# Writing the attention's work in its final order on every engine of a fused transformer block

## The chip, the cores and the metric

The kernel runs on one core of a Trainium2 chip. A core has five engines that run side by side, each with its own stream of instructions: TensorE (PE, matrix products into PSUM), VectorE (DVE), ScalarE (ACT), GpSimd (POOL) and SyncE (SP), which here only issues DMA transfers. The metric is the device time of one launch in microseconds (us). Every stream is fixed when the program is compiled; engines wait for each other by semaphores.

## The reference

One transformer block on a sequence of 2048 rows of width 1024, all in float32:

```python
x = x + layernorm(attention(layernorm(x)))     # 16 heads of 64, rotary q and k, causal softmax
x = x + layernorm(ffn(layernorm(x)))           # silu(x Wg^T) * (x Wu^T), then Wd^T; 2752 inner columns
# q, k, v = y @ Wq, y @ Wk, y @ Wv;  out = softmax(q k^T / 8, masked) v;  attention = out @ Wo
# Wg, Wu, Wd come as 4-bit codes: NF4[codes] * scales, one scale for each block of 64
```

## The kernel before

**Numbers.** Every float32 operand of a product is split into a rounded high part and a remainder (`split`, L125: a ScalarE copy, then a VectorE subtraction), and a product takes three matmuls, high by high, high by remainder, remainder by high.

**Stages.** A start-up makes the normalised and transposed first 512 rows and q, k, v of four head pairs. Then comes one long loop over *steps* (L651) which holds the whole attention and much of what surrounds it; this is what the change is about. After it come the last four projection tiles, the feed-forward's gate and up products, and its down product.

**The step loop.** A unit of work is 128 keys of one head against 512 queries; there are 640 units, one a step, from step 0, and 12 steps ahead of them. In each step things are written in this order of rank: loads of q, k and v for later heads (rank 0, `load_q`, `load_k`, `load_v`); the unit's scores s, two or three matmuls into one of three PSUM banks "S", and their exponential on ScalarE (rank 1, `probabilities`); one matmul for the row maxima of a later head, into a bank "T", with its VectorE reduction (rank 2, `maxima`); filling (rank 3); the weighted sum o of the unit three steps back (rank 4, `weighted`); the split of s into pw (rank 5, `parts`), which frees the bank of s.

**Filling.** `rest` is a Python generator that yields one matmul at a time, or GAP to end the step's share; the table `FILL` says how many matmuls are to be spent by which step. It makes q, k and v of the other head pairs (`qkv`: for each of q, k, v a run of 24 matmuls, then the copy t1, the weight split for the next group, the rotary products t1 and sh on VectorE and GpSimd, the split hl, and its store to DRAM), `values` (transposes of v), and, from about step 440 on, the first 12 tiles of the output projection (`project_out`, each two runs of 24 matmuls; its input is `attended`, the attention's sums af times their reciprocals rt, split into ah and af; its output goes through `residual`, two layer norms and the residual sum). `other_x` runs beside it and makes the other rows' normalised transposes. `looked_up` turns 4-bit codes into weights with eight linear pieces; four such lookups are put into the last steps.

**Buffers.** Tags name rings of SBUF slots (`SLOTS`, L72). The ones that matter here: f4, four slots of 4 KB a partition (weight rows wf and wof, hl, vo, af, ah, mp), pb, two slots (x rows, y, x1), pw, three slots (tables, rt, xs, lookup codes), xc and pa (x tiles, weights).

**Order.** The matmuls are chained by `chain` (L418) in the order written. For every other engine and for the DMA queue, a scheduler picks the order when the program is compiled: it replays the program with modelled durations and takes, on each engine, what is ready by its model, earlier written work first. The order it picks is then fixed: an engine that comes to an instruction whose input isn't there stands still.

Of the kernel before, what the change touches and what calls it, by code (L numbers as in the profile page):

```python
# [20 lines left out]
S = 2048  # L21
# [18 lines left out]
FILL = ((-12, 0), (14, 304), (130, 912), (290, 1520), (430, 2128), (438, 2128), (643, 2704))  # L40
# [19 lines left out]
def block_kernel(ctx, tc, x, wq, wk, wv, wo, gu_codes, gu_scales, d_codes, d_scales, cos_sin, out):  # L60
# [56 lines left out]

    def mm3(o, w, xx, first, last):

        r = T.matmul(o, lhsT=w[:, 0], rhs=xx[:, 0], start=first, stop=False)  # L120
        T.matmul(o, lhsT=w[:, 0], rhs=xx[:, 1], start=False, stop=False)  # L121
        T.matmul(o, lhsT=w[:, 1], rhs=xx[:, 0], start=False, stop=last)  # L122
        return r
# [5 lines left out]
    def ln_stats(row):  # L129
        st = small.tile([P, 2, 6], F32, tag="st", name="st")  # L130
        for i in range(2):
            V.bn_stats(st[:, i, :], row[i])
        mv = small.tile([P, 2], F32, tag="mv", name="mv")
        V.bn_aggr(mv, st.rearrange("p a b -> p (a b)"))
        ve = small.tile([P, 1], F32, tag="ve", name="ve")
        V.tensor_scalar(ve, mv[:, 1:2], EPS, None, ALU.add)  # L136
        rs = small.tile([P, 1], F32, tag="rs", name="rs")
        G.tensor_tensor(rs, ve, nhalf, ALU.pow)  # L138
        nb = small.tile([P, 1], F32, tag="nb", name="nb")
        V.tensor_scalar(nb, mv[:, 0:1], rs, -1.0, ALU.mult, ALU.mult)  # L140
        return mv[:, 0:1], rs, nb

# [42 lines left out]

    def x_rows(r, tag):

        xt = slot(tag, [P, E], F32, "xt")
        load(xt, x[r * P : (r + 1) * P, :])
        mean, rs, _ = ln_stats(halves(xt))  # L190
        V.tensor_scalar(xt, xt, mean, rs, ALU.subtract, ALU.mult)
        return xt
# [7 lines left out]
    def load_x(c, kps):  # L200
        tiles = []
        for kp in kps:
            tiles.append(slot(X_TAGS[c][kp], [P, 4, 2, 2, P], FR, "xc"))
            load(f32(tiles[-1]), xd[c][:, kp])
        return tiles
# [8 lines left out]
    def make_x(c, t, xt):  # L214

        for g in range(0, KE, 4):
# [6 lines left out]
            load(xd[c][:, g // 2 : g // 2 + 2, t], f32(xs))  # L223
            yield GAP

    def qkv(m, c, ws, xs, tab, ramp=False, following=None, before=(), after_n=None):


        cs = slice(c * 512, (c + 1) * 512)
        for n in range(3):  # L230
            w = ws[n]
            o = bank("S" if ramp and n != 1 else "F", "qkv")
            if following:
                wf = load_w(n, following[1])
# [10 lines left out]
            if following:  # L245
                following[0][n] = split_w(wf, following[2])
            if n < 2:
# [5 lines left out]
                hl = slot("f4", [P, 2, 512], FR, "hl")  # L253
                split(hl[:, 0, :], hl[:, 1, :], t1)
                if n == 0:
                    load(qs[m][:, :, cs], f32(hl))
                else:
                    for a in range(2):
                        load(ks[m][a][:, :, cs].rearrange("a d s -> d a s"), f32(hl[a * D : (a + 1) * D]))
            if after_n:  # L260
                after_n(n)
# [4 lines left out]
        def values():  # L266
# [5 lines left out]
            for a in range(2):  # L272
                split(vo[:, a, :, 1], vo[:, a, :, 0], src[:, a])
            load(
                vs[m][:, :, 4 * c : 4 * c + 4].rearrange("a p t n -> p a (t n)"),
                f32(vo.rearrange("p a t l d -> p a (t l d)")),
            )
            done.add((m, c))
# [16 lines left out]
    def startup():  # L295
        nonlocal behind
        for m in range(STARTUP):
            ws[m + 2] = [None] * 3 if m + 2 <= STARTUP else None
            following = ws[m + 2] and (ws[m + 2], m + 2, ("w", "pa", "w", "w")[m])
            behind = yield from qkv(m, 0, ws[m], xs, tab, True, following, behind)  # L300
# [4 lines left out]
    def looked_up(codes, s0, s1, rows, line0="ol"):  # L305
# [6 lines left out]
        load(sc[D:], s1.partition_broadcast(D))  # L312
        l0 = slot(line0, [P, 512], F32, "l0")
# [12 lines left out]
        V.scalar_tensor_tensor(m, line(L6), 0.0, m, ALU.min, ALU.min)  # L326
        l8 = line(L8)
        V.tensor_tensor(p, l8, line(L10), ALU.max)
        V.tensor_tensor(p, p, line(L12), ALU.max)
        V.tensor_tensor(p, p, line(L14), ALU.max)  # L330
        V.scalar_tensor_tensor(m, p, 0.0, m, ALU.max, ALU.add)
        V.tensor_tensor(m, m, sc, ALU.mult)
        return m

    def gate_up_weights(it, line0="ol"):
# [4 lines left out]
        def columns_of(k0):  # L340
# [3 lines left out]
            m = looked_up(  # L344
# [4 lines left out]
        return (it, wt, w), [partial(columns_of, k0) for k0 in range(0, KE, kk)]  # L349
# [35 lines left out]
    def load_q(n, h, J):  # L385

        m, r, cs = h // 2, h % 2, slice(J * 512, J * 512 + 512)
        assert (m, J) in done, (h, J, step, spent)
# [35 lines left out]
    mx_of, later = {}, []  # L424

    def maxima(h, J, j, i):
# [12 lines left out]
        if (j, i) == (3, J):  # L439
# [12 lines left out]
            later.append((3, row))  # L452
# [30 lines left out]
    def weighted(u, h, J, kb):  # L483
# [13 lines left out]
        load(at[J][:, h], y)  # L497
        done.add(("at", h, J))
        if h == 2 * KE - 1 and J < NC - 1:
            reciprocals(J)  # L500

    def prep_wo(k, tag):
        wf = slot("f4", [P, E], F32, "wof")
        load(wf, wo[k * P : (k + 1) * P, :])
        t = slot(tag, [P, 2, E], FR, "wo")
        A.copy(t[:, 0], wf)
        (V, G)[k % 2].tensor_tensor(t[:, 1], wf, f32(t[:, 0]), ALU.subtract)
        return t[:, :, :512], t[:, :, 512:]
# [3 lines left out]
    def reciprocals(J):  # L512
# [3 lines left out]
        V.reciprocal(r, r)  # L516
        load(rcp[J].rearrange("h (a d) -> (h a) d", a=8), r)

    def attended(t):
# [6 lines left out]
        for a in range(2):  # L526
            one = rcp[t // 4][:, cs].rearrange("(k a) n -> a k n", a=2)[a : a + 1]
            load(rt[a * D : (a + 1) * D], one.to_broadcast([D, KE, P]))
        V.tensor_tensor(rt, f32(af), rt, ALU.mult)
        hi = slot("f4", [P, KE, P], FR, "ah")  # L530
        split(hi, af, rt)
        return hi, af

    def project(t, y, a2, beside):

        for n in range(2):
            o = bank("FT"[n] if beside else "FSS"[(2 * t + n) % 3], "pj")
            for k in range(KE):
                yield T.matmul(o, lhsT=a2[0][:, k], rhs=wot[k][n][:, 0], start=k == 0, stop=False)  # L539
                yield T.matmul(o, lhsT=a2[0][:, k], rhs=wot[k][n][:, 1], start=False, stop=False)  # L540
                yield T.matmul(o, lhsT=a2[1][:, k], rhs=wot[k][n][:, 0], start=False, stop=k == KE - 1)  # L541
            A.copy(y[:, n * 512 : (n + 1) * 512], o)  # L542
            yield GAP

    def residual(t, y, xt):

        rows = slice(t * P, (t + 1) * P)
        load(xt, x[rows, :])
        normalize(y, y, ln_stats(halves(y)))
        G.tensor_tensor(xt, xt, y, ALU.add)  # L550
        load(x1d[rows, :], xt)
        normalize(y, xt, ln_stats(halves(xt)))

    def project_out(t, a2, beside):
        y = slot("pb", [P, E], F32, "y")
        yield from project(t, y, a2, beside)
        residual(t, y, slot("pb", [P, E], F32, "x1"))
        load(yd[t], y)
# [3 lines left out]
    def other_x():  # L562
        tiles = [(c, t) for c in range(1, NC) for t in range(4)]
        ready = [x_rows(4, "pb")]
        for n, (c, t) in enumerate(tiles):
            ready += [x_rows(4 * i + j, "pb") for i, j in tiles[n + 1 : n + 2]]
            yield GAP
            while c > 1 and (0, c - 1) not in done:
                yield GAP
            yield from make_x(c, t, ready.pop(0))  # L570
            if t == 3:
                done.add(("x", c))

    def rest():

        xs_, tab_, w, values, ahead = xs, tab, ws[STARTUP], behind, []
        for g in range(STARTUP, len(groups)):
            m, c = groups[g]
            if m == 0:
                while ("x", c) not in done:  # L580
                    yield GAP
                xs_ = [*ahead, *load_x(c, range(len(ahead), 4))]
# [3 lines left out]
            if m == KE - 2 and ("x", c + 1) in done:  # L586
                ahead = load_x(c + 1, range(2))
            if g == len(groups) - 2:
                wot[0] = prep_wo(0, "pa")
            following = [None] * 3  # L590
            last = g + 1 == len(groups)

            def wo_after(n):
                wot[n + 1] = prep_wo(n + 1, "w")

            one = qkv(
                m, c, w, xs_, tab_, False, None if last else (following, groups[g + 1][0], "w"), values, wo_after if last else None
            )
# [7 lines left out]
        for k in range(4, KE):  # L606
            wot[k] = prep_wo(k, "xc")
        yield from values
        assert all(("at", h, J) in done for h in range(2 * KE) for J in range(BESIDE // 4))
        ready = [attended(0)]  # L610
        for _ in range(8):
            yield GAP
        for t in range(BESIDE):
            ready += [attended(i) for i in range(t + 1, min(t + 2, BESIDE))]
            yield from project_out(t, ready.pop(0), True)
# [25 lines left out]
    for i, make in enumerate(first_steps):  # L641
        put(612 + 5 * i, 5, make)
# [7 lines left out]
    fill, beside = rest(), other_x()  # L650
    for step in range(min(work), max(work) + 8):  # L651
        want = np.interp(step, *zip(*FILL))
        for n, f in [e for e in later if e[0] <= 1]:
            f()
        later[:] = [(n - 1, f) for n, f in later if n > 1]
        for rank in range(6):
# [12 lines left out]
            for e in work.get(step, ()):  # L669
                if e[0] == rank:  # L670
                    e[2](*e[3])
    for _ in fill:
        pass

# [56 lines left out]
    for t in range(BESIDE, NT):  # L731
        ready += [attended(i) for i in range(t + 1, min(t + 2, NT))]
        project_now(t, ready.pop(0))
        steps[t - BESIDE]()
# [10 lines left out]
    for it in range(1, NIT):  # L745
# [3 lines left out]
        if it + 1 < NIT:  # L749
            now, steps = gate_up_weights(it + 1)  # L750
            todo.append(now)
            for step in steps:
                step()
# [156 lines left out]
```

## Time and profile before

| | before |
|---|---|
| median of three runs | 3168.86 us (3168.83 to 3170.29) |
| profiled execution, its own time | 3181.73 us |
| its span, first to last instruction | 3180.0 us |
| TensorE, VectorE, ScalarE, GpSimd busy | 3059.7, 2092.3, 1831.7, 532.4 us |
| matmuls | 14272 |
| moved by DMA | 554.69 MB, 174 GB/s over the span |
| mean granted TensorE clock | 0.982 |

A line of the profile names a source line, an engine, an operation and out<-in by the program's names; `PE s L466 <- DVE pw L127` means that TensorE's matmul into s at line 466 waited for VectorE's write of pw, which is issued in the helper at line 127. A matmul's busy time is modelled and overlaps its neighbour's, so a full TensorE shows as no idle time between matmuls, not as a sum of durations. Idle time of an engine that isn't waited for costs nothing.

### The profile page before, as it was taken

To read this page: it belongs to the slowest core of one execution; us is meant where nothing else is said; L and a number is where in the kernel's file an instruction comes from. 1 tells how busy PE (TensorE), PEld (TensorE's weight loads), DVE (VectorE), ACT (ScalarE), POOL (GpSimd) and SP (SyncE) were. 2 spreads that over 40 slices of the span, in tenths; PEclk is the share of its full clock that TensorE was granted. 3 is DMA by queue.
4 is the path that set the end of the run, shared out by engine and by line. 5 is a ranking of instruction groups with operands and counts; after the bars stand their busy time and mean duration, and the time that the engine had idled before them with its cause. 6 is when DMAs were issued, how large, how long until landed. Compare 5 with 4: busy or idle time off the path is not lost.

```text
span 3180.0 us, 41427 instructions
## 1 busy us (share of the span) xinstructions
PE 3059.7 (96%) x14272; PEld 2450.1 (77%) x14272; DVE 2092.3 (66%) x3809; ACT 1831.7 (58%) x3318; POOL 532.4 (17%) x430
## 2 busy tenths in 40 slices
PE   8799999999999998999997899999999999999998
PEld 6588877777777776776676788888888888888887
DVE  5546766766656666676676697677666678957422
ACT  3355666666656666666674586566555567757311
POOL 7443433232333331110001100000000000000000
PEclk9899999999999999999999999999999999999999
DMA  6888866676556656565535433222222325867785
GB/s 195 263 242 236 264 186 203 202 207 176 161 174 187 175 159 182 147 188 159 143 104 159 168 119 106 101 100 99 93 92 95 106 100 179 280 218 250 265 292 204
DMA packets 373394, 554.69 MB, mean 174 GB/s; under 512 B 25216, under 2 KB 238208, under 8 KB 357312
## 3 DMA queue, kind: packets, MB, share of 16 engines
q1 hardware_dynamic: 373184, 552.04, 56.2%
q8 instruction: 113, 1.85, 0.3%
q14 instruction: 97, 0.79, 0.1%
HBM read 410.12 MB, written 141.82 MB: 174 GB/s over the span
## 4 chain that ended last, share of the span: by engine, by line
PE 71%; DMA 4%; DVE 3%; ACT 1%; issue 1%; SPq 1%; POOL 0%; DVEq 0%; POOLq 0%; ACTq 0%
PE bk L121 14%; PE bk L122 14%; PE bk L120 14%; PE s L466 3%; PE mx L432 3%; PE s L467 3%; PE o L491 3%; PE o L490 3%; PE o L492 3%; PE qkv L237 2%; PE qkv L239 2%; PE qkv L238 2%; DMA af<-at 1%; PE pj L541 1%; PE pj L539 1%; PE pj L540 1%
## 5 line engine op out<-in xcount | busy, mean ns | idle before, releaser
L319 ACT ACTIVATE ln<-cs,bias 128x512 f32<-128x512 f32 x910 | 612.3, 718 | 123.2 <-DVE mp L325 40.4
L438 DVE TENSOR_REDUCE mxs<-mx 128x1 f32<-128x512 f32 (+3 forms) x640 | 386.0, 606 | 239.5 <-PE mx L432 145.3
L120 PE MATMUL bk<-x,wt 128*128 128x512 f32 x1376 | 536.6, 391 | 5.9 <-ACT y L542 3.3
L121 PE MATMUL bk<-x,wt 128*128 128x512 f32 x1376 | 537.7, 391 | 1.4 <-DVE x L127 1.4
L122 PE MATMUL bk<-x,wt 128*128 128x512 f32 x1376 | 537.0, 390 | 0.0
L470 ACT ACTIVATE s<-s 128x512 f32<-128x512 f32 (+3 forms) x640 | 331.7, 520 | 315.6 <-PE s L467 188.9
L127 DVE TENSOR_TENSOR pw<-s,pw 128x512 fp32r<-128x512 f32 (+3 forms) x640 | 383.8, 605 | 140.8 <-ACT pw L126 136.2
L183 POOL TENSOR_TENSOR w<-wf,w 128x512 fp32r<-128x512 f32 x192 | 252.3, 1324 | 668.0 <-ACT w L182 550.3
L126 ACT CAST pw<-s 128x512 fp32r<-128x512 f32 (+3 forms) x640 | 332.3, 523 | 51.3 <-PE o L491 35.7
L138 POOL TENSOR_TENSOR rs<-ve,nhalf 128x1 f32<-128x1 f32 x64 | 40.7, 636 | 1865.4 <-DVE ve L136 1831.6
L237 PE MATMUL qkv<-xc,w 128*128 128x512 f32 x768 | 310.5, 406 | 1.4 <-ACT t L244 0.9
L238 PE MATMUL qkv<-xc,w 128*128 128x512 f32 x768 | 308.2, 401 | 0.0
L239 PE MATMUL qkv<-xc,w 128*128 128x512 f32 x768 | 307.6, 401 | 0.0
L120 PEld LDWEIGHTS bk<-x,wt 128*128 128x128 f32 x1376 | 259.1, 189 | 60.1 <-ACT y L542 3.8
L121 PEld LDWEIGHTS bk<-x,wt 128*128 128x128 f32 x1376 | 259.4, 189 | 56.3 <-DVE x L127 2.6
L122 PEld LDWEIGHTS bk<-x,wt 128*128 128x128 f32 x1376 | 259.3, 188 | 54.0 <-DVE wt L127 0.3
L466 PE MATMUL s<-q,ka 128*128 128x512 f32 (+3 forms) x640 | 242.8, 379 | 36.2 <-DVE pw L127 36.2
L432 PE MATMUL mx<-ka,q 128*128 128x512 f32 (+3 forms) x640 | 246.8, 387 | 21.6 <-DVE xs L127 11.0
L121 PE MATMUL bk<-wd,it 128*128 128x512 f32 x672 | 261.5, 389 | 0.0
L120 PE MATMUL bk<-wd,it 128*128 128x512 f32 x672 | 261.5, 389 | 0.0
L122 PE MATMUL bk<-wd,it 128*128 128x512 f32 x672 | 261.3, 389 | 0.0
L467 PE MATMUL s<-q,kb 128*128 128x512 f32 (+3 forms) x640 | 236.6, 370 | 0.0
(126 smaller groups left out, 5439.9 us busy)
## 6 DMA issues: line engine op xcount, KB each, us to landing
it<-ind SPq DMA_DIRECT2D x84, 1024.0 KB
ind<-hl SPq DMA_DIRECT2D x84, 512.0 KB
va<-vs SPq DMA_DIRECT2D x160, 256.0 KB
cs<-in_gu_codes SPq DMA_DIRECT2D x86, 256.0 KB
cs<-in_gu_scales SPq DMA_DIRECT2D x172, 128.0 KB
wf<-in_wq SPq DMA_DIRECT2D x32, 512.0 KB
wf<-in_wk SPq DMA_DIRECT2D x32, 512.0 KB
wf<-in_wv SPq DMA_DIRECT2D x32, 512.0 KB
```

The costliest lines, as they stand in the source:

```text
L120: r = T.matmul(o, lhsT=w[:, 0], rhs=xx[:, 0], start=first, stop=False)
L121: T.matmul(o, lhsT=w[:, 0], rhs=xx[:, 1], start=False, stop=False)
L122: T.matmul(o, lhsT=w[:, 1], rhs=xx[:, 0], start=False, stop=last)
L126: A.copy(hi, src)
L127: V.tensor_tensor(lo, src, f32(hi), ALU.subtract)
L237: yield T.matmul(o, lhsT=w[k][:, 0], rhs=xx[0], start=k == 0, stop=False)
L238: yield T.matmul(o, lhsT=w[k][:, 0], rhs=xx[1], start=False, stop=False)
L239: yield T.matmul(o, lhsT=w[k][:, 1], rhs=xx[0], start=False, stop=k == KE - 1)
L319: A.activation(ln, c8, AF.Identity, bias=bias_of[ab], scale=ab[0])
L432: chain(T.matmul(s, lhsT=q[:, 0, j * P : (j + 1) * P], rhs=ka[:, b:e], start=True, stop=not diag))
L438: V.tensor_reduce(mx[:, j, i : i + 1], s, AX.X, ALU.max, negate=True)
L466: chain(T.matmul(s[:, cs], lhsT=ka[:, ks_], rhs=q[:, 0, cs], start=True, stop=False))
```

## The change

Inside the step loop, each engine's instructions, SP's DMA issues included, are tied in the order in which they are written: after every step `in_order` links each new instruction to the one before it on its engine. So that the written order can be taken as it stands, many pieces are written some steps later or earlier: `defer(n, f)` calls f at the start of the n-th step from then. Outside the loop `defer` calls at once. In particular:

- q, k, v: the rotary split `rotated` comes three steps after its products, its stores one step after that; the stores of v, of the transposed x and of the attention's sums come one step after their writers; `load_q` asks for these marks.
- weights: `load_ahead` loads wf two runs of 24 matmuls ahead of its split, where it was one; Wo's rows (`load_wo`) are loaded apart from their split (`prep_wo`); x tiles are loaded in four pieces each.
- layer norms: `ln_stats` is cut into `ln_sums` and `ln_shift`, written a step apart; the parts of `residual` are spread over several steps; `other_x` loads a tile's rows, sums them and normalises them in different steps.
- projection: `load_attended` (loads) is written at the start of the tile before, `divide` in its middle, the split one step after; x1 is loaded in the middle of the tile, into pw where it was pb.
- lookups: four stages each, in the steps 604 + 8i, +4, +6 and +8, where all of one lookup was written in step 612 + 5i.
- `FILL` gets two more points around step 432.

```diff
-FILL = (..., (430, 2128), (438, 2128), (643, 2704))
+FILL = (..., (430, 2128), (432, 2132), (440, 2140), (643, 2704))
+    def defer(n, f):
+        if pacing:
+            later.append((n, f))
+        else:
+            f()
+    def in_order(start):
+        traced = nc.cur_bb.bb.instructions
+        dep = mybir.DependencyInfo(mybir.DependencyClass.NoSync, mybir.DependencyReason.DATA)
+        for i in traced[start:]:
+            if i.engine in newest:
+                tc.add_manual_dep(i, newest[i.engine], dep, reason="order")
+            newest[i.engine] = i.name
+        return len(traced)
...
-    def load_x(c, kps):
...
-            load(f32(tiles[-1]), xd[c][:, kp])
+    def load_x(c, kps, pace):
+        tiles = [slot(X_TAGS[c][kp], [P, 4, 2, 2, P], FR, "xc") for kp in kps]
+        for n in range(4 * len(kps)):
+            f = partial(load, f32(tiles[n // 4][:, n % 4]), xd[c][:, kps[n // 4], n % 4])
+            if pace:
+                defer(1 + n // pace, f)
+            else:
+                f()
...
+        def rotated(n, t1):
+            hl = slot("f4", [P, 2, 512], FR, "hl")
+            split(hl[:, 0, :], hl[:, 1, :], t1)
+            def store():
...
+            defer(1, store)
-                hl = slot("f4", [P, 2, 512], FR, "hl")
-                split(hl[:, 0, :], hl[:, 1, :], t1)
+                defer(3, partial(rotated, n, t1))
...
-        V.tensor_tensor(rt, f32(af), rt, ALU.mult)
-        hi = slot("f4", [P, KE, P], FR, "ah")
-        split(hi, af, rt)
-        return hi, af
+        return af, rt, slot("f4", [P, KE, P], FR, "ah")
+    def divide(af, rt, hi):
...
+        V.tensor_tensor(rt, f32(af), rt, ALU.mult)
+        defer(1, lambda: split(hi, af, rt))
...
     def residual(t, y, xt):
...
-        load(xt, x[rows, :])
-        normalize(y, y, ln_stats(halves(y)))
-        G.tensor_tensor(xt, xt, y, ALU.add)
-        load(x1d[rows, :], xt)
-        normalize(y, xt, ln_stats(halves(xt)))
+        sums = ln_sums(halves(y))
+        def add():
+            normalize(y, y, ln_shift(*sums))
+            defer(1, lambda: G.tensor_tensor(xt, xt, y, ALU.add))
+            defer(3, again)
+        def again():
+            load(x1d[rows, :], xt)
+            two = ln_sums(halves(xt))
+            defer(1, lambda: normalize(y, xt, ln_shift(*two)))
+            defer(2, lambda: load(yd[t], y))
+        defer(1, add)
...
+            def at_start(n):
+                load_ahead(3 * g + n + 4)
+            def at_end(n):
+                if last:
+                    prep_wo(n + 1, "w")
+                    load_wo(n + 4)
+                else:
+                    following[n] = split_w(wfs.pop(3 * g + n + 3), "w")
...
-        put(612 + 5 * i, 5, make)
+        for j, at_ in enumerate((0, 4, 6, 8)):
+            put(604 + 8 * i + at_, 5, next, stages, None)
...
+    pacing.append(True)
     for step in range(min(work), max(work) + 8):
...
+        traced = in_order(traced)
```

## The prediction

> **What bounds the kernel now.** I read busy time by stretch first, to see where TensorE is not full. Columns: stretch and length in us, busy us of TensorE, its weight load, VectorE, ScalarE and GpSimd (instructions in brackets), granted TensorE clock, DMA share, GB/s.
>
> ```profile
> 78.00:160.00 82.00, 60.47 (x264) 48.69 (x262) 43.58 (x89) 27.16 (x59) 40.25 (x33) 0.83 0.85 264
> 160.00:400.00 240.00, 234.48 (x1296) 193.35 (x1295) 143.86 (x303) 138.39 (x313) 101.03 (x78) 0.99 0.83 246
> 400.00:860.00 460.00, 454.87 (x2301) 354.37 (x2300) 304.77 (x562) 292.56 (x598) 145.47 (x109) 1.00 0.65 189
> 860.00:1200.00 340.00, 333.93 (x1622) 258.35 (x1620) 222.08 (x387) 210.03 (x412) 108.87 (x81) 0.99 0.61 172
> 1200.00:1420.00 220.00, 202.30 (x931) 150.88 (x930) 149.04 (x266) 135.54 (x245) 24.29 (x16) 0.95 0.61 170
> 1420.00:1665.00 245.00, 229.45 (x1048) 170.40 (x1047) 173.63 (x317) 163.33 (x292) 24.78 (x20) 0.96 0.50 143
> ...
> 1845.00:3180.00 1335.00, 1325.87 (x5850) 1097.58 (x5848) 888.52 (x1572) 736.20 (x1164) 9.14 (x16) 1.00 0.47 159
> ```
>
> The last stretch, the feed-forward, is TensorE end to end and the change does not touch it. The attention, 78 to 1665 us, has every other engine at 10 to 71% and TensorE idle for 71.5 us (lengths less busy times). What it waits for, in that window (us in total, times, longest):
>
> ```profile
> PE s L466 <- DVE pw L127: 36.2, 16, 6.1
> PE mx L432 <- DVE xs L127: 11.0, 3, 6.9
> PE mx L432 <- DVE mxs L438: 10.5, 8, 4.8
> PE pt L220 <- DVE mxs L438: 5.6, 2, 4.7
> ```
>
> Few and long. VectorE is only the messenger. The timelines of ScalarE and TensorE around the second longest show who is late:
>
> ```profile
> 871.75 1.08 ACT L470 ACTIVATE s<-s 128x512 f32<-128x512 f32 x2
> 878.67 1.14 ACT L182 CAST w<-wf 128x512 fp32r<-128x512 f32 x2 [5.84 <-DMA wf<-in_wv]
> 879.71 1.06 ACT L126 CAST pw<-s 128x512 fp32r<-128x512 f32 x2
> ...
> 874.60 0.40 PE L492 MATMUL o<-pw,va 128*65 128x512 f32 x1
> 881.07 0.79 PE L466 MATMUL s<-q,ka 128*128 128x512 f32 x1 [6.08 <-DVE pw L127]
> 881.66 0.63 PE L467 MATMUL s<-q,kb 128*128 128x512 f32 x1
> ```
>
> ScalarE reached a weight split whose load had not landed; the casts of finished probabilities stood behind it for 5.84 us, and TensorE ran out of free banks. The matmuls after it take 0.63 us instead of 0.39: the clock is granted at half there (877.3 to 884.1). I looked in this way at every TensorE gap of the attention, and ScalarE's waits name the same few culprits:
>
> ```profile
> ACT hl L126 <- POOL t L252: 37.8, 32, 4.3
> ACT ah L126 <- DVE rt L529: 24.5, 10, 6.7
> ACT w L182 <- DMA wf<-in_wv: 22.1, 9, 5.8
> ACT y L542 <- DMA x1d<-x: 15.1, 3, 7.4
> ACT wo L506 <- DMA wof<-in_wo: 10.2, 4, 7.7
> ```
>
> **The Trainium skill.** "PSUM — Partial Sum Buffer", section "Engine vs sequencer instructions", says the queues of ScalarE, VectorE and GpSimd are strictly first in, first out; the 5.84 us above agree. "TensorE: Matmul & The Clock Gate", section "Part 1: The HAM clock gate", says an idle window of about 3.4 us halves the clock until a busy one has passed. The trace agrees on sizes: half clock comes in pieces of 3.41 and 6.83 us, each after a gap; it also shows it at 228.8 us, after a gap of only 1.85 us. "DMA: Bandwidth & Descriptors", "Rules for kernel authors", advises to issue a DMA early and wait late; in the trace that wf was issued at 866.9 and landed some 11.7 us later, beside a 1 MB xc load.
>
> **The change part by part.** Its form is an order; its substance is a longer lead or a later place for each culprit. The attention has about 655 steps in 1587 us, so a step is 2.42 us.
>
> (1) Weight loads. load_ahead starts wf two units of 24 matmuls before its split instead of one (a unit is some 5 to 6 steps, so 12 us more). The xc loads come in 256 KB pieces, a group's first eight one or two a step. Gaps fed by wf: 6.9 (at 110 us), 1.85 (225), 6.1 (875): **14.8 us**.
>
> (2) Rotary halves (hl) are cast three steps, 7.3 us, after their matmuls. GpSimd needs 2 x 1.32 (w) + 1.63 (sh) + 1.29 (t) = 5.6 us, plus 1.2 for the copy and cast ahead: 6.8, just in time. Gap: **4.7** (104 us). The LN parts (bn_stats a tile behind their load) and the reciprocal four steps behind its sums: 2.2 (285 us) and 1.4 (674 us), **3.6**.
>
> (3) Wo rows are loaded a unit or a step ahead: 3.7 + 1.6 + 3.75 = **9.1** (1204 to 1219 us).
>
> (4) x1 moves from pb to pw, so y no longer waits for the x1d store: 4.8 + 3.0 = **7.8** (1324, 1366 us).
>
> (5) af and rt are loaded at a tile's start and divided half a tile (8.6 steps, 20 us) later, the split one step after. Their waits at 1239, 1457, 1494, 1541, 1570: 0.6 + 1.95 + 4.5 + 1.5 + 3.8 and 0.25 at 1609, **12.6**.
>
> Sum: 14.8 + 4.7 + 3.6 + 9.1 + 7.8 + 12.6 = **52.6 us** of the 71.5. What is left (3.8 at 78, 4.0 at 144, 2.7 at 616 to 620, 3.2 in the table lookups at 1643, small ones) has no part aimed at it.
>
> Half clock: by the stretch table it costs up to 82 x 0.17 + 240 x 0.01 + 340 x 0.01 + 220 x 0.05 + 245 x 0.04 = 40.5 us, but that counts idle time too; the 168 matmuls that start inside it lose 33 us. It goes with the gaps: 33 x 52.6 / 71.5 = **24**. Gain: 76.6 us.
>
> What it adds. SP: 12 xc loads become 48, 36 more issues of about 0.5 us, 18 us over a queue that stands 494 us waiting for TensorE to free va rooms; hidden. The stores that move (32 qs, 64 ks, 32 vs, 24 xd, 64 at, 12 x1d, 12 yd, about 0.3 to 0.6 us of issue each) stand a step behind their writers on SP, past that step's q, ka, kb and va loads, whose own lead is five to eight steps; bounds -5 to 5, I take 0. At the start of a 512-column group eight pieces (2 MB) go at once: 8.5 us at 246 GB/s + 4 us of issue against six steps (14.5 us) of cover; 0 to 12 us over three groups, I take 3. If the cover goes, qkv waits directly. The four f4 buffers hold Wo rows when the last hl is due: one store's landing, 0 to 5, I take 3. The lookups (604 + 8i) want an f4 buffer while two tiles hold all four; by the fill rate 2.78 a tile ends at 610 and 627, so the lookups of 608 and 624 stop VectorE, with the remainders of the next steps' pw behind it and TensorE's s behind those, for two or three steps: 3 to 6 us instead of today's 3.2; I take +1. The order itself on all engines, not shown in this trace: from -15 (the leftover gaps partly go) to +40; I take +4, since ScalarE may be late: the gaps above are mostly 2 to 4 us shorter than ScalarE's own idle time, so about 3 us are covered. The moved stores, copies and normalisations are the same instructions on engines with 25% or more to spare. The stretch from 1665 to 1845 keeps its code: 0. Sum: **+11**.
>
> 76.6 - 11 = 65.6 less. The profiled execution took 3181.7 us around its span of 3180.0, which is 12.9 above the median of 3168.9; taken to the median, 3168.9 - 65 = **3104 us**.
>
> **Rivals.** (a) *Half of it*: the waits re-form behind the same few buffers (four f4, two pb, three pw), since a longer lead holds a buffer longer: two wf, an hl and a vo fill f4. Half of 76.6 less 11 is 27: 3142 us. For it: f4 is full by count. Against: wf landings of 12 us fit in two units of 13. (b) *Slower: written order makes one late piece stop everything.* Place: ScalarE at the end of each of the 84 + 24 units, where copy, two casts and hl precede the exponentials, each waiting for another engine. Price: 1.5 us a unit past the cover, 108 x 1.5 = 160, less the gain 76, plus 20 of clock: about 3270; with one unit in two, about 3183. It decides when the lateness passes the 3 us of cover, that is when GpSimd's 6.8 us become over 10. For it: GpSimd's chain has only 0.5 us to spare before the cover. Against: it is 32 to 49% busy up to 1200 us. (c) *The change does not do it*: the landings are late because DMA engines are full (0.83 to 0.85 busy until 400 us), so a new order moves the same waits; 3165. But the waits of 860 to 1665 come at shares of 0.50 to 0.61.
>
> **How the numbers follow.** Forecast 0.52, its own range 3070 to 3125; (a) 0.25; (b) 0.19; (c) 0.04. About 0.2% is what a measurement can tell from no change. Faster: forecast and (a), 0.77; same: (c) and the seam of (a) and (b), 0.04; slower: (b), 0.19. The range runs from 3055 (leftover gaps and their clock go too: 19 + 9 more, and some of the 25 us idle after 1665) to 3185, the mild end of (b).
>
> **What would show it.** Right: TensorE's idle time in the attention near 25 to 35 us, the stretch before 1420 and 1665 at a clock of 0.99; no ScalarE wait for wf, wof or x1d over 2 us; hl waits on GpSimd under 1 us each. Step 5 is wrong if ah or rt still wait for af. Wrong as a whole: many waits of 1 to 3 us of TensorE on pw or mxs in every unit, or GpSimd's t as ScalarE's first releaser.

## Result: 4.2% slower, and the profile after

The kernel after takes **3301.9 us** (median of four runs, 3295.8 to 3311.2); in the same runs the kernel before takes 3169.1. The ratio is 1.042 (95% interval 1.039 to 1.045). The forecast was 3104 us with a range of 3055 to 3185: wrong in sign. The profiled execution took 3298.7 us around a span of 3296.9; it is 117 us longer than the profiled execution before (3181.7), where the medians differ by 133.

I read the profile after in the order of the prediction, busy time by stretch first (stretch and length in us; busy us of TensorE, weight load, VectorE, ScalarE, GpSimd, instructions in brackets; granted clock, DMA share, GB/s). The attention now ends near 1787 us, so the later stretches are longer than before's.

```profile
160.00:400.00 240.00, 221.18 (x1208) 180.92 (x1208) 143.66 (x283) 127.07 (x296) 96.09 (x73) 0.97 0.79 225
400.00:860.00 460.00, 425.25 (x2110) 329.50 (x2109) 292.43 (x524) 265.42 (x548) 138.49 (x104) 0.97 0.68 187
860.00:1200.00 340.00, 309.21 (x1453) 235.73 (x1452) 199.53 (x342) 185.50 (x371) 95.11 (x70) 0.95 0.54 151
1200.00:1540.00 340.00, 326.05 (x1531) 245.69 (x1530) 239.70 (x419) 215.78 (x395) 55.86 (x41) 0.97 0.63 173
1540.00:1790.00 250.00, 211.59 (x929) 152.89 (x928) 165.82 (x300) 151.09 (x275) 19.71 (x17) 0.93 0.49 134
...
1970.00:3297.00 1327.00, 1315.96 (x5804) 1088.69 (x5802) 878.88 (x1555) 728.79 (x1152) 9.14 (x16) 1.00 0.46 159
```

The feed-forward (last row) is what it was. From 400 to 1200 us, where TensorE had been idle for 11.2 us of 800, it is now idle for 65.5. From the first maxima matmul to the last weighted sum, worked out from the matmul starts of both traces, the attention grew from 1564.6 to 1687.9 us, by 123.3: TensorE's gaps in it from 67.7 to 157.0 (+89.3), its time at half clock from 78.5 to 139.9 us, which costs up to half of the difference (30.7; what of it lies in gaps costs nothing more). Those two together make up to 120.0 of the 123.3.

The chain of work that ended last (shares of the span) and TensorE's waits from 78 to 1790 us (us in total, times, longest) name one transfer:

```profile
PE 61%; DMA 9%; DVE 4%; ACT 2%; SPq 1%; issue 1%; POOL 0%; DVEq 0%; POOLq 0%; ACTq 0%
PE bk L143 13%; PE bk L142 13%; PE bk L144 13%; DMA q<-qs 6%; PE mx L499 2%; PE o L557 2%; PE s L533 2%; PE o L558 2%; PE o L559 2%; PE s L534 2%; PE qkv L289 2%; PE qkv L288 2%; PE qkv L290 2%; PE pj L627 1%; PE pj L626 1%
```

```profile
PE mx L499 <- DMA q<-qs: 86.9, 30, 7.4
PE s L533 <- DVE pw L149: 24.8, 16, 3.2
PE pt L256 <- DVE xt L681: 24.3, 9, 4.8
PE mx L499 <- DVE mxs L505: 7.5, 7, 2.1
```

`mx L499` is the maxima matmul, `q<-qs` the load of a head's q: 30 waits, about one for every second of the 64 pairs of a head and a query block. The trace before shows no wait of TensorE for q. ScalarE's waits, which carried the prediction, did change as meant for the weights:

```profile
ACT hl L148 <- POOL t L303: 34.2, 26, 4.1
...
ACT ah L148 <- DVE rt L614: 14.0, 9, 4.5
...
ACT w L210 <- DMA wf<-in_wv: 4.7, 1, 4.7
...
ACT w L210 <- DMA wf<-in_wq: 2.7, 1, 2.7
```

The waits for wf fell from 36.8 us (22.1 for Wv, 8.5 for Wk, 6.2 for Wq) to 7.4, and those for x1d and wof are gone; ah on rt fell from 24.5 to 14.0, hl on GpSimd barely. TensorE's `s <- pw` fell from 36.2 to 24.8. The named culprits mostly went, and something larger came.

What is behind a q wait? SP's timeline after (start, duration, issue), then TensorE's at the same place:

```profile
879.61 0.64 SPq L470 DMA_DIRECT2D kb<-ks  x1
880.30 0.84 SPq L464 DMA_DIRECT2D ka<-ks  x1
881.18 0.48 SPq L465 DMA_DIRECT2D q<-qs  x1
881.71 0.66 SPq L466 DMA_DIRECT2D q<-qs  x1
```

```profile
885.36 0.22 PE L536 MATMUL s<-mask_k,ident_r 128*128 128x128 f32 x1
892.01 0.80 PE L499 MATMUL mx<-ka,q 128*128 128x512 f32 x1 [6.43 <-DMA q<-qs]
892.60 0.63 PE L288 MATMUL qkv<-xc,w 128*128 128x512 f32 x1
```

The last q load leaves SP at 882.4. TensorE comes to the matmul that needs it at 885.6, and the matmul starts only at 892.0, 9.6 us after the end of the issue, which stands behind kb and ka on the queue. The matmul itself and the one after it take 0.80 and 0.63 us: half clock. In the trace before, the last q issue of one head at this place ends at 881.0 and its first maxima matmul runs at 918.4, 37.5 us later (SP's timeline, then TensorE's):

```profile
879.10 1.16 SPq L398 DMA_DIRECT2D q<-qs  x1
880.31 0.65 SPq L399 DMA_DIRECT2D q<-qs  x1
```

```profile
918.44 0.45 PE L432 MATMUL mx<-ka,q 128*128 128x512 f32 x1
```

That is a habit, not an accident. The time from the end of a head's last q issue to its first maxima matmul, called its lead from here on (median, by query block J of 512 rows), is worked out from each trace, with the sum of TensorE's gaps before these matmuls. The last row takes each gap off, and so ends where TensorE came to the matmul:

| | J=0 | 1 | 2 | 3 | gaps, us |
|---|---|---|---|---|---|
| before | 14.3 | 26.9 | 42.5 | 59.3 | 3.9 |
| after | 9.0 | 9.1 | 9.0 | 12.5 | 85.9 |
| after, less the gap | 9.0 | 8.8 | 6.6 | 11.4 | |

The code says why: `put(at_, 0, load_q, ...)` writes the load at step `at_`, and the first maxima at `at_ + 4`. Four steps are 9.7 us by the prediction's 2.42 us a step. In the kernel before, the scheduler was free to issue q as soon as its ring had room, however late it was written. In written order SP cannot issue it before the stores that are written ahead of it, and these wait for their writers: L566 stores the attention's sums, L319 v, L276 k. SP's waits from 78 to 1725 us, and then from 874 to 884 us, ahead of the q above:

```profile
SPq L566 <- ACT yl L563: 247.1, 35, 19.4
SPq L319 <- DVE vo L149: 198.6, 21, 25.4
...
SPq L276 <- DVE mxs L505: 75.7, 18, 11.6
```

```profile
SPq L566 <- ACT yl L563: 14.5, 1, 14.5
SPq L276 <- DVE mxs L505: 1.8, 1, 1.8
```

These waits are idle time of SP and cost nothing by themselves; I read them as what ties the queue to the step. For the q above the queue cost part of the four steps too: SP stood at a store until 875.2, then had a va load, two stores of k with their own 1.8 us of waiting, kb and ka ahead of q, and of the 9.7 us only 3.2 were left when TensorE came.

### The profile page after: what moved, and what is told of

It is laid out like the page before. It is cut to its first block, busy times and chain, and to the rows that moved or that the text cites. A ratio compares the mean times of both kernels' runs of the same rounds, so it can differ in the third digit from the quotient of the medians.

```text
span 3296.9 us, 41383 instructions
## 1 busy us (share of the span) xinstructions
PE 3092.4 (94%) x14272; PEld 2463.3 (75%) x14272; DVE 2117.8 (64%) x3793; ACT 1825.1 (55%) x3318; POOL 534.8 (16%) x430
## 4 chain that ended last, share of the span: by engine, by line
PE 61%; DMA 9%; DVE 4%; ACT 2%; SPq 1%; issue 1%; POOL 0%; DVEq 0%; POOLq 0%; ACTq 0%
PE bk L143 13%; PE bk L142 13%; PE bk L144 13%; DMA q<-qs 6%; PE mx L499 2%; PE o L557 2%; PE s L533 2%; PE o L558 2%; PE o L559 2%; PE s L534 2%; PE qkv L289 2%; PE qkv L288 2%; PE qkv L290 2%; PE pj L627 1%; PE pj L626 1%
## 5 line engine op out<-in xcount | busy, mean ns | idle before, releaser
L149 DVE TENSOR_TENSOR pw<-s,pw 128x512 fp32r<-128x512 f32 (+3 forms) x640 | 391.0, 611 | 198.2 <-ACT pw L148 194.4
L211 POOL TENSOR_TENSOR w<-wf,w 128x512 fp32r<-128x512 f32 x192 | 270.0, 1428 | 763.0 <-ACT w L210 762.9
L499 PE MATMUL mx<-ka,q 128*128 128x512 f32 (+3 forms) x640 | 251.5, 396 | 101.5 <-DMA q<-qs 86.9
L533 PE MATMUL s<-q,ka 128*128 128x512 f32 (+3 forms) x640 | 243.3, 380 | 25.0 <-DVE pw L149 24.8
L557 PE MATMUL o<-pw,va 128*65 128x512 f32 (+3 forms) x640 | 239.4, 374 | 1.0 <-ACT yl L563 0.8
```

The costliest lines, as they stand in the source:

```text
L149: V.tensor_tensor(lo, src, f32(hi), ALU.subtract)
L499: chain(T.matmul(s, lhsT=q[:, 0, j * P : (j + 1) * P], rhs=ka[:, b:e], start=True, stop=not diag))
```

## Experiments

My theory: the four written steps between q's load and its first use are too short, and the order on SP makes them binding. Rival 1: the order on the engines, above all the normalised rows xt written in the same step as their transposes. Rival 2: the DMA engines are full, or the moved pieces (wf, Wo, af, x1) are what costs.

**e1: q early.** `load_q`, which loads ka and q, is written up to eight steps earlier for J of 1 to 3, as far as the rings allow; order unchanged.

```diff
-        put(at_, 0, load_q, n, h, J)
+        early_q = at_ - AHEAD * (J > 0)     # AHEAD = 8; then not before its q and ka slots are free
...
+        put(early_q, 0, load_q, n, h, J)
```

> The changed kernel with one thing different: the loads of ka and q (load_q) are written up to 8 steps earlier for heads of the second to fourth 512 queries, as far as their rings have room (4 to 8 steps in nearly all 48 heads); the maxima stay where they are. Theory 1 (the queue in written order issues q only four steps, 9 us, ahead of its first matmul): the 87 us of gaps of mx on q nearly all go, with about a third of that in half clock: 3302 - 80 - 27 = 3195 us. Rival A (written order on ScalarE and VectorE is what costs; the q wait is only the last of several): the gaps reappear on pw and mxs, above 3270. Rival B (the DMA engines are too busy, q lands late however early it is issued): above 3270, and the wait on q stays.

Measured: 3186.9 us, 1.007 of before (1.006 to 1.009): 115 us of the 133 lost are back. ka moves with q in this run, so it does not separate the two; TensorE waits for q, the last of them on the queue. q's waits fall from 86.9 us to 7.5, half clock from 139.9 us to 68.3. TensorE's waits of e1, 78 to 1790 us:

```profile
PE s L533 <- DVE pw L149: 27.0, 16, 4.6
PE pt L256 <- DVE xt L681: 24.3, 9, 4.8
PE mx L499 <- DVE mxs L505: 8.5, 8, 2.1
PE mx L499 <- DMA q<-qs: 7.5, 4, 3.0
```

and one stretch, after and then e1:

```profile
640.00:1220.00 580.00, 525.64 (x2485) 400.23 (x2484) 355.11 (x615) 322.50 (x649) 164.05 (x122) 0.96 0.57 162
```

```profile
640.00:1220.00 580.00, 573.83 (x2811) 441.26 (x2810) 395.18 (x685) 363.33 (x727) 181.32 (x134) 1.00 0.64 179
```

In e1 the DMA share is higher (0.64 against 0.57) and the waits are gone: full DMA engines were not what made q late. And the written order, with q early, runs this stretch with TensorE idle for 6 us of 580.

**e2: a step between xt and its transposes**, in `other_x`.

```diff
                 V.tensor_scalar(nxt, nxt, mv[:, 0:1], rs, ...)
+                yield GAP
```

> The changed kernel with one more GAP in other_x, between the normalisation of a tile's rows on VectorE and the transposes of that tile on TensorE, which the change had put into one step. Theory 1 and a second, smaller cause (TensorE waits in the same step for xt, 9 waits of 24.3 us in all): 24 of gaps and 8 of half clock go, 3270 us. Rival A: no change beyond 5 us, as VectorE is late anyway.

Measured: 3299.0 us, 1.042 (1.040 to 1.044), no gain. The place was right: VectorE normalises for 1.75 us just when TensorE wants the rows (VectorE's, then TensorE's timeline, after):

```profile
306.07 1.75 DVE L681 TENSOR_SCALAR xt<-xt,mv,rs 128x1024 f32<-128x1024 f32 x1
```

```profile
307.96 1.09 PE L256 MATMUL pt<-ident_r,xt 128*128 128x128 f32 x4 [4.85 <-DVE xt L681]
```

In e2 the xt waits fall from 24.3 to 6.4 us, by 17.9. q's rise from 86.9 to 96.5, a new wait of the transposes for xs takes 6.4, and TensorE's gaps are in all what they were (157.9 us, after 157.0). What TensorE gains at xt it spends at other waits, the larger part of it at q.

**e3: e1 and e2 together.**

> The changed kernel with both earlier edits: load_q up to 8 steps earlier for the heads of the second to fourth 512 queries, and the GAP between the normalisation of xt and its transposes. With q early the xt gaps (24.3 us there too) are the largest single wait left. Theory 1 with its second cause: 3187 - 24 - 8 = 3155 us, about the kernel before. Rival (as in the run with the GAP alone, 3299: the time comes back as other waits): above 3180.

Measured: 3165.6 us, 1.000 (0.999 to 1.001). With q early the same GAP is worth 21 us (3187 to 3166). Here the second wait had a price only once the first was gone.

**e4: SP left to the scheduler; e5: no order at all; e6: order on SP alone.** These split the order in two.

```diff
-            if i.engine in newest:
+            if i.engine in newest and i.engine != mybir.EngineType.SP:     # e4
+            if i.engine in newest and i.engine == mybir.EngineType.SP:     # e6
...
-        traced = in_order(traced)                                          # e5
```

> The changed kernel with SP's DMA issues left out of the written order: only TensorE, VectorE, ScalarE and GpSimd are tied, the queue's order is the scheduler's again. Theory 1: q is issued 20 us and more ahead as before, its gaps go, 3302 - 107 = 3195 us, or a little more if stores now stop the queue. Rival A: stays above 3270.

> The changed kernel without any written order: every deferral, longer lead and split stays, in_order is not called, and the scheduler orders all engines but TensorE, and the queue. Theory 1 (the order of the queue costs, the moved pieces gain as reckoned): the gaps of before on wf, wof, x1d and af stay gone and q is early: 3100 to 3150 us. Rival C (the moved pieces are what costs, by buffers held longer): above 3230. Rival A: 3100 to 3170 too.

> The changed kernel with the written order on SP's DMA issues alone; VectorE, ScalarE and GpSimd are the scheduler's. Theory 1 (the written order of the queue costs by itself, 3302 - 3177 = 125 us): 3130 + 125 = 3255 us, with mx waiting for q. Rival A (only the tie of all engines together makes the queue late): below 3180.

| order on | neither | engines | SP | both |
|---|---|---|---|---|
| kernel | e5 | e4 | e6 | after |
| us | 3130.0 | 3176.6 | 3309.2 | 3301.9 |
| ratio | 0.989 (0.988 to 0.990) | 1.004 (1.002 to 1.005) | 1.045 (1.043 to 1.046) | 1.042 (1.039 to 1.045) |
| lead of q, J=3 | 54.9 | 55.1 | 13.1 | 12.5 |

The order on SP costs 179 us alone (54 more than I expected), the order on the engines 47; together they cost 172, less than the sum, which fits waits that hide each other as in e2. The lead goes with SP's order. TensorE's first waits of e6, and then of e5:

```profile
PE mx L499 <- DMA q<-qs: 110.2, 34, 7.9
PE s L533 <- DVE pw L149: 21.6, 17, 3.1
```

```profile
PE s L533 <- DVE pw L149: 17.4, 14, 5.5
PE pv L312 <- ACT xs L148: 6.4, 1, 6.4
```

e5, all moved pieces without the order, is 35 us faster than before in the same runs: gaps 40.2 us instead of 67.7, half clock 30.7 instead of 78.5.

**e16: q two steps later**, the other direction.

```diff
+        put(at_ + 2, 0, load_q, n, h, J)
```

> The changed kernel, order and all, with load_q two steps later: two steps ahead of the first maxima instead of four, so each of 64 heads has 4.8 us less. Theory 1: the 30 heads that waited wait 4.8 us longer (144 us), the others 2 to 4 us (100), and half clock follows with a quarter: about 3600 us. Rival B (the landing is set by DMA load, not by the lead): within 50 us of 3302.

Measured: 3402.1 us, 1.075 (1.073 to 1.076), 100 more than after, a third of what I expected. `PE mx L499 <- DMA q<-qs` takes 170.3 us in 41 waits, 83 more; half clock 238.9 us, 99 more. Direction and cause hold. The size failed in two ways: 41 of the 64 loads were waited for and not all, and a wait grew on average from 2.9 to 4.2 us, by 1.3 and not by 4.8.

**e7: e3 with the order only in steps 20 to 599. e9: e3 with no order. e12: e3 with the order on SP alone. e13: e2 with the order in steps 20 to 599 on the engines, not SP.**

```diff
-        traced = in_order(traced)
+        traced = in_order(traced) if 20 <= step < 600 else len(nc.cur_bb.bb.instructions)   # e7, e13
```

> The changed kernel with load_q early, the GAP, and the written order only in the steps 20 to 599: start-up and the table lookups are ordered by the scheduler. Where q was early, the stretch from 640 to 1220 us showed hardly a gap over 1.3 us, while the lookups cost some 18 us of gaps and 6 of clock and the first 80 us some 20. If those are due to the written order: 3155 - 24 - 10 = 3120 us. Rival: the scheduler's own start and end bring their own gaps as in the kernel before: 3145 us and more.

> Control: no written order at all, with load_q early and the GAP. Theory 1: where the scheduler orders the queue, it takes q as soon as its ring has room, so the step in which it is written does not matter: 3130 us, as without the two edits. Rival (an early q helps by itself, by DMA load or rings): more than 10 us off 3130.

> The written order on SP's DMA issues alone, with load_q early and the GAP; the other engines are the scheduler's. Theory 1 (the queue's order costs only through q's lead): the q gaps go, and the af and xt loads, which the scheduler had issued late in the runs without order (18 us of gaps), come as written: 3309 becomes 3105 to 3125 us, the fastest so far. Rival (the queue's order has further waits): above 3150.

> The written order on TensorE, VectorE, ScalarE and GpSimd in the steps 20 to 599 only, SP free, with the GAP. The order on these engines in all steps had cost 3177 against 3130 without. If that was xt written ahead of its transposes in one step and the lookups (24 + 8 and 18 + 6 us): 3121 us. Rival (an order of engines costs in the middle too): above 3150.

Measured: e7 3142.4 us (0.994; 0.992 to 0.995), e9 3137.1 (0.991; 0.990 to 0.993), e12 3171.0 (1.001; 1.000 to 1.002), e13 3136.5 (0.991; 0.989 to 0.992). From e3 to e7, taking the order off both ends of the loop is worth 23 us; from e7 to e9, off its whole middle, 5. So the written order of 580 steps is nearly as good as the scheduler's, once q and xt have their lead. The same holds for the order on the engines alone, which costs 47 us in e4 and in e13, with the GAP and without the ends, no more than 7 (3136.5 against 3130.0 in e5). In e9 the earlier place of q changes nothing about its lead (12.4, 27.8, 41.9, 54.5 us by J, in e5 12.6, 28.0, 42.1, 54.9): the scheduler does not mind where q is written. e7 and e13 came 22 and 15 us above what I expected (3120, 3121); for e7 the rival, that the scheduler's own start and end bring gaps of their own (3145 and more), was the nearer one. The ends are where the start-up's work and the lookups lie. At the lookups of e1 (ScalarE's timeline) the linear pieces stand ahead of an exponential and of the cast that frees its bank, and TensorE's waits in 1560 to 1680 us follow:

```profile
1613.37 2.20 ACT L374 ACTIVATE ln<-cs,bias 128x512 f32<-128x512 f32 x3 [1.55 <-DVE cs L370]
1615.48 0.58 ACT L537 ACTIVATE s<-s 128x512 f32<-128x512 f32 x1
```

```profile
PE s L533 <- DVE pw L149: 18.7, 11, 3.2
```

e12 missed: I expected SP's order with q early to be harmless (3105 to 3125 us). It costs 34 us against e9, in gaps of 71.3 instead of 48.8 us. Its VectorE, ordered by the scheduler, waits up to 6.9 us for xt rows and 6.5 us for rt that the queue issues later than the scheduler's model had them; I read that as the cause, and no run isolates it.

**e10, e11, e14, e15, e17: moved parts undone, all without order.** e10 loads wf one unit ahead, e11 puts x1 into pb, e14 loads Wo's rows at their split, e15 divides and splits af where it is loaded; e17 does all four. **e18** calls what `defer` was given at once, the row of maxima apart.

```diff
-                load_ahead(3 * g + n + 4)
+                load_ahead(3 * g + n + 3)                                   # e10, e17
...
-        xt = slot("pw" if beside else "pb", [P, E], F32, "x1")
+        xt = slot("pb", [P, E], F32, "x1")                                  # e11, e17
...
-        for k in rows:
+        for k in ():                                                        # e14, e17
...
-        wf = wof.pop(k)
+        wf = slot("f4", [P, E], F32, "wof")                                 # e14, e17
+        load(wf, wo[k * P : (k + 1) * P, :])
...
-            yield from project_out(t, (now[2], now[0]), True, nxt and partial(divide, *nxt))
+            if nxt:                                                         # e15, e17
+                V.tensor_tensor(nxt[1], f32(nxt[0]), nxt[1], ALU.mult)
+                split(nxt[2], nxt[0], nxt[1])
+            yield from project_out(t, (now[2], now[0]), True, None)
...
-            later.append((n, f))
+            f()                                                             # e18
```

> No written order, and wf loaded one unit of 24 matmuls ahead of its split, as in the kernel before, instead of two. It prices the first part of the predicted gain (14.8 us of gaps and about 7 of half clock). If the part was reckoned right: 3130 + 22 = 3152 us. Rival (the two f4 buffers that the longer lead holds cost as much as it brings): 3125 to 3137.

> No written order, and x1 of the tiles beside the attention in pb again, so that the next y waits for the store of x1d. It prices the fourth part (7.8 us of gaps and about 4 of half clock): 3130 + 12 = 3142 us if reckoned right; 3125 to 3133 if the earlier load of x1 has already taken that wait away.

> No written order, and the rows of Wo loaded where they are split, as in the kernel before. It prices the third part of the forecast gain (9.1 us of gaps, about 4 of half clock): 3130 + 13 = 3143 us if reckoned right; within 5 us of 3130 if the scheduler hides it, as with wf and x1.

> No written order, and the division and the split of af written right behind its load at a tile's start, as in the kernel before. It prices the fifth part (12.6 us of gaps, about 6 of half clock; 8.7 us of such gaps are left in the run without order): 3130 + 10 = 3140 us if the place in the tile is what gains; within 5 us of 3130 if not.

> No written order, and the four large parts undone together: wf one unit ahead, Wo's rows loaded at their split, af divided at its load, x1 in pb. If the gain of 35 us stands on these parts and any one of them can fail alone: back to 3160 to 3170 us. If it comes from the rest (deferred splits and stores, layer norms and lookups in pieces): within 8 us of 3130.

> No written order and no deferral: what defer puts off is written at once (the row of maxima apart, which was put off before too), while the longer leads of wf, wof and af, x1 in pw and the pieces of xc, other_x and the lookups stay. If the gain comes from the deferrals: 3155 to 3170 us. If it comes from the pieces or leads: within 8 us of 3130.

| against before | us | ratio (95%) |
|---|---|---|
| e5, nothing undone | 3130.0 | 0.989 (0.988 to 0.990) |
| e10, wf | 3130.8 | 0.988 (0.987 to 0.990) |
| e11, x1 | 3131.2 | 0.988 (0.986 to 0.990) |
| e14, Wo | 3124.8 | 0.986 (0.984 to 0.988) |
| e15, af | 3131.5 | 0.989 (0.987 to 0.992) |
| e17, all four | 3134.1 | 0.990 (0.988 to 0.992) |
| e18, deferrals | 3134.4 | 0.989 (0.988 to 0.991) |

All intervals overlap. The four parts that the prediction priced at 14.8, 9.1, 7.8 and 12.6 us are worth 4 us together by the medians (13 by the outer ends of the intervals). Under the scheduler the places where these parts are written hardly matter. What they are worth in written order, as in the kernel after, no run shows. The 35 us that e5 gains come from something else among the edits (the pieces of the layer norms and `other_x`, the x tiles in pieces, the lookups in stages), or from the four parts and the deferrals standing in for each other, which no run undoes together; which, stays open.

The fastest kernels seen are this group, about 3130 us, faster than before by 1.1% and than after by 5.2%: the change's pieces without its order.

## Why the prediction was wrong, by its steps

**The failing step is SP's.** The moved stores stand, it says, "a step behind their writers on SP, past that step's q, ka, kb and va loads, whose own lead is five to eight steps; bounds -5 to 5, I take 0." I read k's and v's lead from `put(b - 8, ...)` and `put(b - 5, ...)` and gave it to q, whose first use is the maxima, four steps behind its load and well before the scores at b. Nor did I ask what lead q had in the trace: 27 to 59 us for J of 1 to 3, which written order was bound to cut to about the 9.7 of four steps. The term that I set at 0 measured 115 us (after against e1): q's waits are 79.4 of it, and half clock, 71.6 us shorter in e1, is up to 36.

**"The order itself on all engines"**, which I put at +4 with bounds of -15 and +40, measured +172 (after against e5), with SP's part in it; the engines alone are 47 (e4 against e5): outside my bounds too, if by little. The bound was taken from gaps of a schedule without the order, which says nothing of leads that the order takes away. The cover of "about 3 us" was not general either: in the very gap that the prediction shows, TensorE stood longer (6.08 us) than ScalarE (5.84).

**Parts (1), (3), (4) and (5), 14.8 + 9.1 + 7.8 + 12.6 = 44.3 us**: the waits named did shrink, but under the scheduler the four parts are not worth this price (4 us when all four are undone, e17); in written order they were not tested apart. Each gap was put down to the instruction that was late in one execution of one schedule. When that part's place changes, the scheduler replays the whole, and I take it that another order with about as many gaps comes out: e17 has 46.4 us of them, e5 40.2.

**Part (2), "just in time"**, did not hold: 7.3 us against GpSimd's 6.8 left ScalarE's wait `hl <- t` at 34.2 us in 26 waits, from 37.8 in 32.

**The clock**: the forecast took 24 us for 52.6 us of gaps, 0.46 for each. What the attention's length changed beyond its gaps, for each us of gaps, was (123.3 - 89.3) / 89.3 = 0.38 from before to after, (107.8 - 77.1) / 77.1 = 0.40 from after to e1, (105.9 - 74.3) / 74.3 = 0.43 from after to e16, and (45.6 - 27.5) / 27.5 = 0.66 from before to e5. The rate was about right, the gaps were not. In e5 gaps fell by 27.5 us where I had summed 52.6.

**The sum's base.** The gaps came from an execution 12.9 us above the median, and were taken from the median. Between profiled executions e5 gains 52.6 us (3181.7 to 3129.1), between medians 35. So it seems that some of the idle time that I removed is not there in a usual run.

**The lookups, "+1"**: the written order at the loop's two ends costs 23 us (e3 against e7); how much of that is theirs, the runs do not separate.

**The rivals.** (b), slower, had the right kind: one late piece stops everything in written order. Its place (ScalarE at the end of each unit) was wrong; it was a load on SP's queue, late by up to 7.4 us where (b) asked for 3. (c), full DMA engines, falls for q with e1: higher share, fewer waits. (a), half of the gain, is near what e5 shows (3130 against 3142), but that is a kernel without the order, and no run shows waits that re-form behind the buffers; the nearness is luck. My signal for "wrong as a whole", TensorE waiting on pw or mxs in every unit, did not appear; TensorE waited for the DMA directly.

## What to carry to other kernels

Before an order picked by a scheduler is replaced by a written one, list for every load its lead in the trace (end of issue to first use) and in the written program (steps times the step's length): where the second is shorter than the load takes to land, the engine that uses it waits for the rest. A queue that also carries stores did not make it up here; it took a part of the written lead as well. Price the written order queue by queue, and start with the one whose instructions wait for other engines. A gap in one scheduled trace tells who was late in that schedule, not what moving that piece is worth (44.3 us by the gaps, 4 by e17); try the part alone before adding such gaps up.

## What the runs showed of the hardware

- The q load shown above, 128 and 256 KB behind ka and kb, was used 9.6 us after the end of its issue, with TensorE waiting for it, in a stretch with a DMA share of 0.54; with median leads of 17 to 26 us for J of 1 to 3 (e1) TensorE waited once in those 48 loads.
- The Trainium skill, "DMA: Bandwidth & Descriptors", section "Rules for kernel authors", advises to issue early and wait late. These runs put a size on it: two steps less (about 5 us) over the 64 q loads cost 100 us (e16), up to eight steps more for 48 of them brought 115 (e1).
- With each us of TensorE's gaps the attention grew by more than that us: by 0.38 to 0.43 us more in the three pairs with the written order, by 0.66 from before to e5 (the clock paragraph above has the working).
